# New order tables for a 32-batch graph-network kernel, and the timing rules of the recorder that carries them

## The chip, the cores and the metric

The kernel runs on one core of a Trainium2 chip. The metric is device time in microseconds (us) of one execution. A core has five engines that run side by side, each through its own instructions strictly in the order in which the program lists them: TensorE (PE in the profile; its weight loads are listed apart as PEld), VectorE (DVE), ScalarE (ACT), GpSimd (POOL) and SyncE (SP, here only a queue of transfers). An instruction waits until the data and the buffers it needs are ready; everything behind it on its engine waits too. So the order of the instructions on each engine decides how well the engines overlap.

## The reference

Four graph layers run one after the other on 32 independent graphs ("batches") of 512 nodes with 128 features. Each layer takes a layer norm and a ReLU of x, computes its update and adds it to x:

```python
h = jnp.maximum(_layernorm(x), 0.0)
# layer 0: for each node the maximum over its neighbours (adj is 0 or 1, some 16 of 512)
p, q = h @ (W1 - W2), h @ W2
x = x + max over j of relu(p[i] + q[j] + b) * adj[i, j]
# layer 1: four sub-layers; each aggregates along rows and along columns of adj
src_agg = l2norm(adj, 2) @ (nodes @ ws + bs)
dst_agg = l2norm(adj, 1).T @ (nodes @ wd + bd)
f = tanh(concat(src_agg, nodes @ wn + bn, dst_agg) @ wu + bu)
# layer 2: one normalised aggregation, out = adj_n @ (h @ weight) + bias
# layer 3: four times a GRU cell over m = adj.T @ (h @ weight[l])
r, z = sigmoid(...), sigmoid(...); n = tanh(xn + r * hn); h = (1 - z) * n + z * h
x = x + h * mask
```

## The kernel before

Every batch is worked on whole: 512 nodes are four tiles of 128 rows. `batch` (L1847) calls `load`, `prepare`, `gathers`, `layer1` and `layer23`; three functions of `FastWeights` (`first`, `rest`, `last`, L1218 to L1368) prepare the weights. The steps of a batch, with the names that the profile uses:

- `load` and `prepare`: x and the adjacency matrix (`af`) arrive by transfers of the ACT queue. VectorE checks the matrix (`junk`), takes the norm's statistics (`st`, `mv`, `rstd`, `shift`), GpSimd raises rstd to the power -1/2, ScalarE writes `xn`. ScalarE casts the matrix to bfloat16 (`ab`); TensorE transposes it in 16 bfloat16 matmuls (`pat`, 128 columns each), multiplies the features (`pq`) and makes running counts of the neighbours (`pc`), which ScalarE casts (`cc`) and four SP transfers for each tile rearrange (`ccd`). 16 more bfloat16 matmuls of 128 columns (`pkey`) make keys from which VectorE finds the first neighbours (`top`, `at8`), and from those the list `idx`.
- `gathers`: GpSimd issues 28 indirect transfers (`G`, and `gm` for the first of each tile) that fetch neighbours' rows; VectorE keeps the maximum (`gm`). For neighbours beyond the first seven VectorE makes one-hot rows (`oh`; in the first three batches ScalarE makes some, through `far`), TensorE multiplies (`pa`, 32 float32r matmuls of 512 columns) and VectorE keeps the maximum (`acc`). `px` transposes it back; GpSimd adds it to x (`x1`) and issues four loads of the matrix as float32r (`an`).
- `layer1` and `layer23`: the aggregations `pg` (104 float32r matmuls of 512 columns in a batch: each value is split into a high and a low part, `hi` and `lo`), the dense products in float32 (`pu`, `pk`, `phn`, `pxn`: 45 of 512 columns), float32 transposes (`pt`, `pf`, `px`, `ph`), and between them the chain of activations on ScalarE and elementwise work on VectorE and GpSimd (`zc`, `lo`, `shift`). The result `xo` is stored by the ACT queue.

The arithmetic is the same in every batch; only a few groups of operations are split in halves in the first and the last batch.

The order is not written out by hand. All those calls go through `Flow` (L826), which records an operation (`Op`) instead of issuing it, with a cost, an engine and what it depends on. `run` (L1090) gives each recorded operation a due time from a table, `queue_up` (L957) sorts the operations of each engine by due time, and `step` (L1012) then issues the heads of the five queues, one at a time, always the one that can start first by the recorder's own clock. Within an engine the order is therefore that of the due times alone. The recorder's costs decide only three other things: how the engines' instructions are interleaved while the program is built, which of the eight PSUM banks a tile gets (`Share`, L748), and where `clock` (L1062) puts filler: a bfloat16 matmul named `spin`, written where the recorder expects TensorE to idle for more than a microsecond[...].

The tables are text, two characters of difference of three-glyph numbers in hundredths of a microsecond. `FRONT` holds one row for each of the three weight functions and for batches 0 to 7; `MIDDLE` is one row, used for batches 8 to 21, each shifted by `PERIOD`; `BACK` holds batches 22 to 31. A row is a starting time and one number for every operation of that batch.

What the recorder assumes before the change: 0.06 us from one engine to another (`LAT`), 0.25 us more in front of a matmul (`LOAD`), 0.13 us for each semaphore beyond the first that a VectorE, ScalarE or GpSimd instruction has to wait for (`EVENT`), and a port that VectorE and GpSimd hold by turns for some operations (`port`). A matmul costs the same whatever stood before it.

Of the kernel before, what the change touches and what calls it, by code (L numbers as in the profile page):

```python
# [13 lines left out]
F32 = mybir.dt.float32  # L14
F32R = mybir.dt.float32r
# [10 lines left out]
P = 128  # L26
# [11 lines left out]
PERIOD = 81.7354  # L38
# [3 lines left out]
    450.09,  # L42
    (
        "!!!!WQ!+m!0U!/Z!<.!8c!47!2a!=<!@j!A#!Gg!^L!|h!z_!}5!|?#3@#6##DX#FW#JH#e)#xU#xa#y,#z(#vC#"
        "xl#y7#y=$$P#sM#yB#}O$#E$,y#z/#|%#|r$#K$-p#}2#~&$)Y$)v$/&$+K$,1$-b$4_$,]$-,$/0$0Z$2u$4:$5"
        "#$7>$@#$/<$/m$24$39$1+$2e$1=$1k$3j$=8$8Z$>n$1l$67$=i$>=$Qn$7Q$2&$:@$Db$<d$g-$;M$0=$4u$;M"
        "$?r$DQ$Dg%XB#])$2U$9T$9[$9b$:!$<h$6e$6l$6s$7t$85$8~$9;$9M$9i$:*$:~$?1$A9$C|$E>$FF$Hw$K&$"
        "LN$T|$MK$Sj$T/%>2$QU$W7$Md$S&$Tw$^2$V)$bH$XE$cW$Yf$dh$^b$hT$bx$kY$d7$lr$eR$nd$hw$q|$k}$w"
        "$$o6$yB$pD$|?$v,$~S$wG%#t$yf%&+$|b%,<$~v%+p%$:%.[%&M%0#%,_%5u%-z%6k%/?%9R%2V%=#%6<%>h$;_"
        "$>g$B/$@($C+$=R$Ce$H:$Et$Kn$>P$JB$Mp$LZ$O2$Ac$Lr$R@$Oy$S^$G#$P4$VR$SR$Wp$NP$Tp$X[$V$$YU$"  # L50
        "Pq$X2$ZN$Zk$[G$T?$]w$`|$^I$ah$^S$`J$bj$`b$cy$_]$e?$jr$i9$m|$`>$oW$p)$q+$r4$nx$w-$xb$wa${"
        "_$ps$x7$}5$|x$~h$|S$}y%$,%#*%%I$}r%%|%&M%(2%(_%!U%(N%)X%(l%*{%8`%8k%93%9>%?q%A3%Eb%EC%Hq"
        "%E#%-H%ID%9R%:O%#5${$%eH%dg%Oo%LD%L&%KH%Ko%N_%LX%Kh%Nf%Nx%O2%Q(%QS%TJ%Ts%U@%Uj%VC%Z-%iE%"
        "ct%ec%f)%gz%h?%eK%fJ%fy%gc%h@%ho%iA%iW%jl%en%f3%fb%g4%gK%hW%i*%o`%qn%k:%lK%t(%t~%v3%w>%w"
        "I%wT%w`%x7%xz%yI%{3%|!%|Q%}!%}:%}Q%}i&!%%zU%zs%{J%|:%~/%~F&!0&!G&#X&!_&!v&#q&%%&&K&(Z&(|"
        "&)V&)a&*%&,&&+7&-2&-x&.J&/3&/y&16&1e&3@&+M&-I&-a&.3&.b&1M&1|&31&4(&+e&+|&0;&27&3H&4X&5Y&"
        "6k&7t&89&8C&<]&=1&=s&>{&A,&Ab&Ay&BJ&C#&Cj&Ee&Mo&B4&Bb&C;&D,&DC&DZ&Dr&EB&H$&O$&O<&P6&QS&R"
        "f&Sw&Tr&V(&YZ&^W&_i&aH&bX&bo&c5&cc&h<&gq&h)&dO&iS&i1&iL&g(&jf&j{&l;&lP&mD&oG&lw&mm&o}&qL"
        "&p#&w8&wO&wg&w~&xU&xm&y(&}M($f(%d(%z(&4(&T(,O(+|(($((?(-J(-s(,q();(.2(.9(.+(+S(.R(.i(.K("
        "0!(28(3k(48(0;(4o(5W(5D(5O(5Z(5l(69(7>(89(93(9J(9b(9y(:4(:K(:c(:z(;K(<i(>%(=z(?7(@:(;W(>"  # L60
        "}(>n(@6(A2(A$(B%(Bn(Cx(D&(DI(Dl(E1(F%(Dw(Eq(G&(G>(GU(Gm(H((H?(HV(Hn(I?(KL(Lu(L^(N*(P`(IV"
        "(JQ(M|(OK(Pw(QQ(R?(S^(Un(Uy(V((W-(WN(X`(V3(WO(Y](Z.(ZE(Z](Zt([/([F([^(]/(_<(^B(`M(a-(c<("
        "`M(b/(a_(cR(dA(d5(e7(f!(gM(gX(gd(go(h4(i[(gz(i0(k$(k<(kS(kk(l=(lT(ll(m&(mT(nm(oh(o~(px(q"
        "q(ml(pb(pm(qs(ro(ra(sc(tO(uW(uc(un(uy(wn(wS(v>(w9(xE"
# [6 lines left out]
            "!!!!(?!(S!(+!(h!)7!!S!)X"  # L71
# [3 lines left out]
        2.69,  # L75
        (
            "!!Z!.r!1P!/F!2$!-m!2U!3*!3Z!4/!0|!4`!/w!54!5e!69!6j!0K!.A!:y!;>!=U!!B!<0!=O!<:!@:!B2!B^!"
            "<D!@D!!!!%Z!;(!;I!<(!<p!+N!<>!<`!==!>*!*m!=S!=u!>S!@N!>i!>j!?#!@<!?O!?O!?q!&m!;I!@D!@f!A"
            "P!B<!<`!Ag!BM!C+!CW!=u!CH!Cj!DH!Du!D^!D_!E%!FW!Fp!FB!G?!?O!@f!Fl!Fw!Go!IV!HW!JE!Bs!I5!I@"
            "!J*!K=!Lg!My!Cj!L!!Ki!LO!M8!M{!NJ!MN!MN!Me!N5!P%!Ny!Y=!FU!Gh!Q!!Q3!QO!Qz!S(!SR!Rn!T+!Im!"  # L80
            "SG!T#!T/!Un!Vb!Vx!W1!W^!LO!WR!WG!Wu!X:!Y.!Z*!Yp!ZV!YC!YD!YZ!Zh!Z*!ZF!Zs"
# [3 lines left out]
        4.33,  # L85
        (
            "!$G!(H!Y_!az!aX!b4!ao!bT!!!!ad!bT!b>!c*!*5!b)!bI!cf!d+!d{!fq!bv!il!ia!i#!jo!d+!jn!jy!k(!"
            "kI!l=!pC!j1!pE!p;!pP!pr!kI!r3!r>!r(!r`!t[!uW!pr!v|!w+!w6!xb!r`!y|!z+!z6!zW!{X#83!&m!|=!}"
            "q"
# [5 lines left out]
            "!!!!!M!#(!)z!*X!*2!+*!+!!*x!*Q!+I!+c!+y!+[!-3!.N!-K!.%!.x!.$!0p!1w!3:!4A!/E!/[!/r!0,!2e!"  # L95
            "27!32!4^!5p!65!2C!3=!6*!65!7,!2N!3H!5{!6A!8/!2Y!4j!6L!6W!:p!4u!8Y!9k!=Y!6c!7^!:0!:R!Ah!C"
            ".!Fb!Gi!:a!9T!<3!>2!@^!<u!?G!9l!=b!CM!GW!FR!JP!:&!Cd!H,!G&!MF!DH!=:!G1!Lk!_X!S3!I>!;w!<0"
            "!>&!>=!>S!>i!LS!5?!=Q!>O!>V!>^!>{!?g!?f!?m!?s!?z!@R!Ei!BU!B]!Bd!EH!He!K5!F{!G%!GC!GJ!L&!"
            "NG!Q8!T*!QM!GQ!R>!R_!Qf!Wp!TE!S7!US!`/!Vb!bu!X~!d~!Z0!eu!`_!i&!cI!k|!eQ!mv!fm!oK!iJ!qo!l"
            "C!tl!n=!vb!oo!x`!r~!{o!u2!}V!w(#!L!y%#$J!|6#(Z!}z#*H#!o#,7#$m#.5#(}#1~#+O#3t#,}#5I#.X#6}"  # L100
            "!J$!L-!Lr!Lq!MY!Le!N?!PB!P;!QW!J5!MF!PR!RC!Pj!S<!Nr!Pn!RV!Ux!Up!Vr!T2!V@!Wk!Vi!Xd!U;!W#!"
            "Y^!Ye!ZV!TK!VX!Z*![_!]G!_N!X?!Zg!]_!`P!]u!aI!^E!_v!c:!`1!d4!b7!c@!f:!cW!g3!^(!_x!co!h-!g"
            "f!i;!aG!c+!g}!k2!h8!lr!j)!kY!n.!kq!o`!l5!m>!pp!o&!r&!hF!ku!ps!s)!q-!s~!od!rG!tP!u8!th!vv"
            "!x/!x:!xE!yQ#7@#8r#;&#;e#:d#;E!$Z#<>!^Z!])![>!]p!_(!X<!Y+#?Y#?2#>+#?F#?y#?n#>J#@##@7#@L#"
            "@>#Ac#B,#Bc#C0#CX#D3#Dy!u1#C0#CY#DA#E*#EV#Eo#Fw#G(#G@#Gr#H/#H;#HT#K[#F+#G4#GL#GY#Gf#G~#H"
            "G#J!#M!#Ha#Hm#Hy#IA#IM#IY#If#Is#LO#J?#JK#JX#Je#Jq#LS#La#Lm#O@#M1#Nf#Mj#Nr#N:#P.#Pp#PY#Q)"
            "#Qk#Qp#Q{#R^#Ri#R@#T:#S.#SZ#S6#U(#U@#UY#Uf#Ur#V!#V;#Vm#SZ#U4#UM#V/#VG#VT#Va#Vm#Wo#Vy#W*#"
            "W6#WB#WO#W[#X!#X/#XR#X<#XH#XT#Xa#Xn#Xz#Y*#Y6#YY#YC#[1#YO#[=#Y{#Zb#[G#]E#]|#^b#]:#]q#_U#_"
            "a#_,#br#`$#b<#`%#c`#d)#dA#dM#dg#e!#e0#eR#`N#cl#cx#d5#ds#e<#eH#eU#e{#c3#dZ#eb#en#ez#f+#f7"
            "#fC#f~#c@#fO#f]#fi#fu#g$#g2#g>#h=#gJ#je#gW#jq#h&#k@#hR#kl#i)#l;#iT#j2#kV#lg#mD#n*#m~#n-#"  # L110
            "nz#o(#pG#q0#oI#pH#q1#qz#rM#rY#rg#rs#s/#sT#{k#qT#rA#s!#s<#sH#sb#sn#sz#ui#t*#t7#tC#tO#t[#t"
            "i#tu#v<#}4#u$#u1#vj#vv#w>#wJ#wV#wc#|o#z/$#c#|V$$j#}Y$%V#~)$&=#~T$(#$!$$(g$!P$)6$#7$*%$#o"
            "$$>$,A$*R$*~$-4$-5$-?$.($.2$2&$4s$4`$4K$3*$7Y$7K$7R$3I$9:$9g$9B$=>$=V$>v$>M$>#$@!$E?$Ah$"
            "A($GB$GY$Gq$H,$HC$HY$Hq$Ku$My$N3$N`$Nv$Sc$S}$OZ$RD$Uj$VC$T;$Rj$Vq$Vc$Vj$S-$W&$W=$Ww$XS$Y"
            "F$Zy$Xy$[F$[|$_)$]E$]W$]j$]u$^;$_F$`W$aR$aj$b$$b;$bR$bj$c$$c<$cj$e,$f%$f<$g7$h4$cv$gV$g4"
            "$hh$id$ld$kv$nm$ou$p#$q7$qB$qd$rs$p<$r_$sY$t-$tD$t[$ts$u.$uD$u[$v-$x?$yh$yO$zy$|!$v.$w9$"
            "zL${p$|`$}2$~^%!{%$C%$N%%T%%`%&#%(5%$Y%&$%)2%)a%)x%*2%*I%*a%*x%+3%+a%-q%,`%/%%-q%1i%.l%0"
            "A%0(%2)%2t%2z%3v%4b%5l%6q%6|%7+%7L%8?%5w%7e%9Y%9q%:,%:C%:r%;-%;D%;[%<?%=K%>E%>[%?V%@N%<."
            "%?@%?K%@Q%AM%A?%BA%C6%D?%DO%DZ%Df%H$%Gf%G1%GK%HM"
# [5 lines left out]
            "!*T!0>!0v!1.!1B!1w!1i!1p!1b!2:!2L!2c!2S!3y!5E!6f!4y!4B!=f!A#!C,!D+!FB!GZ!L#!L5!L@!]U!L/!"  # L125
            "LP!LV!L[!d{!LJ!Lb!Lg!Mm!f/!Ms!Mx!M~!NJ!h&!N4!ND!NO!Na!hz!dS!b.!rw!vL!e!!eN!kM!s<!tq!uJ!w"
            "5!xk!uH!lD!lr!pG!mV!n+!px!lk!nc!r5!tC!so!uy!mV!qz!zC!vM!tt!rf!o~!w|!zt!{y!{H!y:!jW!l-!o<"
            "!oQ!oh!qM!qc!G@!t4!t;!tB!tI!{_!~c!v5!v<!vB!vI!yK!z`!vP!vW!v_!vf!|y#!n!vm!y5!y<!yC##`#$]#"
            "*7#2|#*L!{<#$r#3[#9*#>4#:8#=%#-D#B7#/9#G-#0k#Ci#2B#F9#Bh#K0#G^#P<#Hy#QW#J+#S4#KR#Uh#P_#Y"
            "=#Qz#[8#SV#]]#V/#_S#Y`#c(#[[#e##^##g,#_v#ht#cK#kw#eF#mk#gN#os#i:#qu#l=#t|#n1#vU#p:#x_!}Y"  # L130
            "#!]#$@#$P#&K#%G#&P#(D#&h#)I!|b!~>#(!#*V#(G#-6#!]#%&#*E#/+#+E#0]#+7#0(#3&#1Y#3p#,@#1~#4i#"
            "2R#5b#*<#.,#3.#6[#4l#7T#/K#2B#5e#9P#6_#<M#;D#>o#?W#?V#@P#=.#@?#AI#AH#DB#3|#9J#D)#HD#G<#I"
            "0#:i#A8#HR#L%#LS#M$#E0#M)#O[#NB#PP#KD#OG#R1#Rg#U+#BV#NI#UI#U}#XK#YQ#Oh#Q&#Yk#ZJ#Z2#[M#]c"
            "#]n#]y#^(#x~#ym#{}#|@#{^#{?!!!#}2#,H#D{#+^#*s$*5$)S#xd$!Z#~z$!2$!F$#r$#d$#k$#]$$/$$D$$($"
            "%Z$%t$&g$(Y$)%$)]$*F$.1$)_$)j$)u$*#$*E$*`$,>$-V$.@$.o$/@$/o$0*$1]$,U$-($-?$-n$.)$/*$/W$3"
            "x$6p$0A$2%$2}$7x$:B$;K$;V$;y$<U$<w$=b$=v$?($?V$@)$@@$@V$@n$A@$An$>1$??$?n$A)$AW$Ao$B*$D,"
            "$Ew$DB$DY$El$G!$I.$J6$JA$JL$JW$Jy$LU$Kw$N%$N=$O&$P>$PU$Qo$R*$R~$L2$Mk$NT$Nl$OU$RA$SS$Te$"
            "UA$LI$La$Pt$RX$Sj$U5$VJ$WZ$Xd$Z@$ZK$^j$_>$`&$a|$co$d1$dH$d_$eO$e~$gi$qs$b>$dv$eg$f9$fP$f"
            "h$g!$h#$k-$lL$ld$uy$vt$x)$y#$zM${H$~{%%I%&Z%*q%*|%++%+6%+w%-e%0I%1>%,p%0B%1g%1n%.n%2u%34"
# [2193 lines left out]
```

## Time and profile before

| | us |
|---|---|
| median of 3 runs (2860.01 to 2862.24) | 2861.26 |
| the profiled execution | 2865.97 |
| its span, from the first to the last instruction | 2864.3 |
| PE, PEld busy | 2784.9, 1727.7 |
| DVE busy | 2491.5 |
| POOL, ACT busy | 1738.8, 1272.7 |

The numbers that follow come from the profiled execution, which took 4.7 us more than the median. "Busy" is the time in which at least one instruction of an engine was under way. Matmuls overlap in their pipeline, so the distance from one matmul's start to the next tells more of TensorE than the duration that a row gives. Nearly all operations are issued by one line, L1048 in `step`, so groups are told apart by the tiles that they write and read, not by line.

The batches leave the core at an even pace for most of the run: the stores of `xo` are issued at 284.5 us for batch 0 and at 2400.1 us for batch 25, which is 84.6 us for a batch, and at 2853.8 us for batch 31.

### The profile page before, as it was taken

The numbers are of one execution on the slowest core, as the hardware profiler recorded it, in microseconds if no ns is written. First come the engines' busy times: TensorE is split into PE (matmuls) and PEld (weight loads), VectorE is DVE, ScalarE is ACT, GpSimd is POOL, SyncE is SP. The second block draws the span as 40 slices with busy tenths as digits, with TensorE's granted clock in tenths as the row PEclk, the third lists the DMA queues.
The fourth block names the chain that finished last, engine by engine and source line by source line (L and its number), as shares of the span: only waits on it lengthen the run. The fifth ranks groups of instructions, "written<-read, shape, count | busy, mean of one in ns | idle before, by whom it ended". The sixth has DMA issues, their size and how long they took to land.

```text
span 2864.3 us, 37049 instructions
## 1 busy us (share of the span) xinstructions
PE 2784.9 (97%) x11230; PEld 1727.7 (60%) x11230; DVE 2491.5 (87%) x5757; ACT 1272.7 (44%) x2622; POOL 1738.8 (61%) x1892
## 2 busy tenths in 40 slices
PE   7899999999999999999999999999999999999997
PEld 4565656665666666566666666666655555656665
DVE  5889999999999999999999999999998998888633
ACT  5744444444444444444444444444444444444333
POOL 3676666666666676666666666666665666655311
PEclk8999999999999999999999999999999999999999
DMA  6654443434344343334343334434333434333100
GB/s 160 121 78 77 73 86 71 84 71 81 73 89 86 65 88 72 77 80 87 72 82 74 79 74 88 87 64 92 72 78 78 88 78 88 57 62 59 35 5 9
DMA packets 188178, 217.60 MB, mean 76 GB/s; under 512 B 28826, under 2 KB 136516, under 8 KB 187972
## 3 DMA queue, kind: packets, MB, share of 16 engines
q0 software_dynamic: 47104, 92.34, 24.4%
q1 hardware_dynamic: 73540, 64.62, 7.6%
q10 hardware_dynamic: 67328, 58.20, 6.6%
q8 instruction: 92, 1.51, 0.2%
q14 instruction: 114, 0.93, 0.1%
HBM read 164.32 MB, written 17.17 MB: 63 GB/s over the span
## 4 chain that ended last, share of the span: by engine, by line
PE 58%; DVE 19%; issue 9%; ACT 5%; POOL 4%; DMA 2%; SPq 1%; DVEq 0%; ACTq 0%; POOLq 0%
PE pg L1048 19%; PE pk L1048 11%; PE pu L1048 9%; DVE acc L1048 6%; PE pa L1048 5%; PE phn L1048 3%; DVE oh L1048 3%; PE pxn L1048 3%; DVE nn L1048 2%; POOL rstd L1048 2%; POOL G L1048 2%; DVE lo L1048 2%; PE ph L1048 1%; PE pf L1048 1%; ACT xn L1048 1%
## 5 line engine op out<-in xcount | busy, mean ns | idle before, releaser
L1048 POOL DMA_INDIRECT G<-qtab,idx x768 | 829.7, 1080 | 522.0 <-DVE gm L1048 259.3
L1048 DVE TENSOR_TENSOR acc<-acc,pa 128x512 f32<-128x512 f32 x992 | 672.9, 678 | 66.6 <-PE pa L1048 44.2
L1048 PE MATMUL pa<-oh,qhl 128*128 128x512 f32 x1024 | 535.3, 548 | 6.1 <-DVE acc L1048 2.1
L1048 PE MATMUL pu<-ag,w 128*128 128x512 f32 (+1 forms) x952 | 452.9, 572 | 0.0
L1048 PE MATMUL pg<-an,hi 128*128 128x512 f32 (+1 forms) x1072 | 446.5, 418 | 0.4 <-DVE lo L1048 0.4
L1048 PE MATMUL pg<-an,lo 128*128 128x512 f32 (+1 forms) x1072 | 428.0, 405 | 0.3
L1048 DVE TENSOR_SCALAR oh<-ccd 128x1024 fp32r<-128x1024 bf16 x492 | 374.5, 771 | 2.8 <-PE pa L1048 1.5
L1048 ACT ACTIVATE xn<-x,shift,rstd 128x128 f32<-128x128 f32 x512 | 223.5, 485 | 221.3 <-POOL shift L1048 211.0
L1048 PE MATMUL pg<-at,hi 128*128 128x512 f32 (+1 forms) x672 | 291.5, 441 | 2.3 <-ACT oh L1048 1.4
L1048 PEld LDWEIGHTS pa<-oh,qhl 128*128 128x128 f32 x1024 | 193.6, 191 | 144.1 <-issue 68.2
L1048 PE MATMUL pg<-at,lo 128*128 128x512 f32 (+1 forms) x672 | 278.9, 418 | 1.0 <-POOL lo L1048 0.8
L1048 POOL TENSOR_TENSOR rstd<-rstd,mhalf 128x4 f32<-128x4 f32 x128 | 190.4, 1488 | 109.5 <-DVE rstd L1048 92.1
L1048 ACT ACTIVATE gate<-pk,bsum 128x512 f32<-128x512 f32 (+1 forms) x264 | 174.6, 674 | 180.1 <-PE pk L1048 178.6
L1048 PE MATMUL pk<-h,g_hh 128*128 128x512 f32 (+1 forms) x528 | 253.3, 585 | 0.7 <-ACT h L1048 0.7
L1048 PE MATMUL pk<-mT,g_ih 128*128 128x512 f32 (+1 forms) x528 | 252.8, 583 | 0.4 <-ACT mT L1048 0.3
L1048 DVE TENSOR_TENSOR gm<-gm,G 128x128 f32<-128x128 f32 x768 | 244.0, 319 | 7.4 <-DMA G<-qtab,idx 6.3
L1048 PEld LDWEIGHTS pu<-ag,w 128*128 128x128 f32 x952 | 171.5, 190 | 123.1 <-issue 96.0
L1048 PEld LDWEIGHTS pg<-an,lo 128*128 128x128 f32 x1072 | 202.8, 189 | 65.2 <-issue 28.2
L1048 PEld LDWEIGHTS pg<-an,hi 128*128 128x128 f32 x1072 | 202.9, 189 | 64.8 <-issue 24.9
L1048 ACT COPY mT<-pg 128x512 f32<-128x512 f32 (+1 forms) x164 | 94.4, 576 | 319.3 <-PE pg L1048 311.4
L1048 POOL DMA_INDIRECT gm<-qtab,idx x128 | 133.3, 1041 | 99.7 <-issue 86.2
L1048 DVE TENSOR_TENSOR ag<-pg,rbc 128x512 f32<-128x512 f32 (+1 forms) x272 | 174.9, 646 | 21.2 <-PE pg L1048 17.8
(177 smaller groups left out, 5241.8 us busy)
## 6 DMA issues: line engine op xcount, KB each, us to landing
ccd<-cc SPq DMA_DIRECT2D x512, 64.0 KB
an<-in_adj_dram POOLq DMA_DIRECT2D x128, 256.0 KB
af<-in_adj_dram ACTq DMA_DIRECT2D x31, 1024.0 KB
x<-in_x_dram ACTq DMA_DIRECT2D x64, 256.0 KB
rbc<-scal SPq DMA_DIRECT2D x32, 512.0 KB
G<-qtab,idx POOLq DMA_INDIRECT x768
qtab<-qn SPq DMA_DIRECT2D x32, 256.0 KB
out_dram<-xo ACTq DMA_DIRECT2D x32, 256.0 KB
```

What stands on the lines that cost most here:

```text
L1048: op.fn(*(real(v) for v in op.args), **{k: real(v) for k, v in op.kw.items()})
```

## The change

The arithmetic and the recorded operations stay as they are. All due-time tables are replaced, and the recorder's assumptions are:

```diff
-PERIOD = 81.7354
+PERIOD = 81.7343
...
-    LAT = 0.06
-    LOAD = 0.25
+    LAT = {"pe": 0.035, "vec": 0.035, "act": 0.035, "pool": 0.09, "sync": 0.035}
+    LOAD = (0.08, 0.09, 0.14, 0.2)
+    SWITCH = {(1, 2): 0.066, (0, 2): 0.006, (3, 2): 0.006}
...
-    EVENT = 0.13
+    YIELD = 0.12
...
+                wide = self.name == "pool" and op == "tensor_scalar" and outs[0].free_size() >= P
+                self.flow.part[-1].port = fast or wide or len(tensors) > 1
+            if self.name == "pool" and (op.startswith("tensor") or "indirect" in op):
+                self.flow.part[-1].kind = not self.flow.part[-1].port
...
         if "pool" in at and ops["pool"].port:
             at["pool"] = max(at["pool"], self.port["vec"])
+        elif "pool" in at and ops["pool"].kind:
+            at["pool"] = max(at["pool"], self.port["vec"] - self.YIELD)
...
-        cost = op.cost + (self.EVENT * max(0, len(need) - 1) if op.engine != "pe" else 0.0)
+        cost = op.cost
         if op.engine == "pe":
-            cost /= self.rate
+            cost = (cost + self.SWITCH.get((self.kind, op.kind), 0.0)) / self.rate
+            self.kind = op.kind
```

Every matmul now carries a kind (0 float32 transpose, 1 bfloat16, 2 float32r, 3 float32), and a float32r matmul behind a bfloat16 one is counted with 0.066 us more. A GpSimd instruction that takes no turn at the port is nevertheless held back until 0.12 us before VectorE gives the port up. Some costs change by a few hundredths (an SP transfer of bfloat16 0.6 instead of 0.48, an indirect transfer 1.0 instead of 1.05, operations on half the partitions 0.11 more, an accumulating ScalarE operation 0.1 less).

The tables have one row more in `FRONT` (batches 0 to 8), `MIDDLE` covers batches 9 to 21, `BACK` has the same ten batches. The order is different on every engine, in all batches. Counted in the order of the built programs:

| | before | after |
|---|---|---|
| matmuls without fillers | 9960 | 9960 |
| VectorE, GpSimd, SP instructions | 6765, 1930, 811 | 6765, 1930, 811 |
| `spin` fillers, all | 209 | 128 |
| `spin` fillers up to the output of batch 0 | 127 | 73 |
| bfloat16 matmul followed by a float32r one, all | 408 | 56 |
| the same in one inner batch | 14 | 1 |
| float32r matmul followed by a bfloat16 one, all | 379 | 136 |
| the same in one inner batch | 12 | 4 |

In an inner batch the 32 bfloat16 matmuls stood mostly one by one among float32r aggregations; in the new order they stand next to float32 products and float32 transposes. At the start, the preparation of layer 1's weights (`wt`, `pwt`, `pw`, and the SP loads that feed it) stood between the steps of batch 0, and now comes after more of them: the SP queue writes all 16 `ccd` pieces of batch 0 before it goes on with those weights, where weight loads stood between the pieces before, and on GpSimd the first `an` load comes after two gathers instead of after eight. ScalarE issues one instruction more in the whole program (3068 instead of 3067): one more load of an activation table, since `low` of the weights now comes behind batch 0's `xn` and `hT`.

## The prediction

> **What bounds the kernel now.** I read the page's busy shares first, then busy time by stretches, then TensorE's timeline from start to start, then the waits.
>
> ```profile
> span 2864.3 us, 37049 instructions
> ...
> PE 2784.9 (97%) x11230; PEld 1727.7 (60%) x11230; DVE 2491.5 (87%) x5757; ACT 1272.7 (44%) x2622; POOL 1738.8 (61%) x1892
> ```
>
> TensorE is busy 97% of the time, VectorE 87%, so TensorE is the bound. But a busy share of overlapping matmuls hides lost time, so I price TensorE's work by distances between starts. Stretches of one batch's length, two of them inner:
>
> ```profile
> core 0: us, PE busy (x) PEld busy (x) DVE busy (x) ACT busy (x) POOL busy (x), PEclk, DMA share, GB/s
> 0.00:84.10 84.10, 62.46 (x290) 38.51 (x290) 52.00 (x141) 52.08 (x120) 34.11 (x74) 0.86 0.61 154
> 84.10:168.20 84.10, 70.51 (x379) 47.86 (x378) 70.44 (x180) 51.41 (x95) 58.95 (x68) 0.94 0.68 110
> ...
> 925.10:1009.20 84.10, 83.80 (x333) 51.53 (x331) 77.98 (x179) 37.64 (x79) 55.00 (x59) 1.00 0.40 79
> 1513.80:1597.90 84.10, 83.80 (x333) 51.60 (x332) 78.10 (x179) 37.65 (x78) 55.05 (x59) 1.00 0.41 79
> ...
> 2775.30:2859.40 84.10, 69.49 (x332) 46.74 (x330) 33.43 (x94) 28.65 (x62) 10.64 (x17) 0.98 0.03 7
> ```
>
> The inner batches repeat to a tenth of a microsecond, and only the first two stretches and the last leave TensorE really idle. Now two places on TensorE's timeline, each with one short matmul among float32r ones:
>
> ```profile
> 1500.00 0.40 PE L1048 MATMUL pa<-oh,qhl 128*128 128x512 f32 x1
> 1500.24 0.23 PE L1048 MATMUL pkey<-ltk,at 128*128 128x128 bf16 x1
> 1500.28 0.48 PE L1048 MATMUL pg<-at,hi 128*128 128x512 f32 x1
> 1500.60 0.39 PE L1048 MATMUL pg<-at,lo 128*128 128x512 f32 x1
> ...
> 1533.80 0.27 PE L1048 MATMUL pt<-ident,xn 128*128 128x128 f32 x1
> 1533.83 0.48 PE L1048 MATMUL pa<-oh,qhl 128*128 128x512 f32 x1
> 1534.14 0.40 PE L1048 MATMUL pg<-at,hi 128*128 128x512 f32 x1
> ```
>
> Float32r matmuls follow each other every 0.23 us. A float32 transpose costs 0.109 (transposes in a row start 109 ns apart), and transpose plus float32r matmul take 1534.14 - 1533.80 = 0.34: nothing extra. A bfloat16 matmul costs 0.056, yet with the float32r one behind it takes 1500.60 - 1500.24 = 0.36, where 0.056 + 0.232 = 0.288 was due.
>
> By such distances an inner batch is: 144 float32r of 512 columns at 0.232 us, 33.4; 45 float32 of 512 at 0.858 (two records of 0.429 each), 38.6; 49 transposes at 0.109, 5.3; 32 bfloat16 at 0.056, 1.8; four `pq` at 0.432 and four `po` at 0.222, 2.6. Sum 81.7. Between the stores of batch 0 and batch 25 a batch takes (2400.1 - 284.5)/25 = 84.6, so 2.9 are lost in each.
>
> With the same prices TensorE's order holds 181 us of work up to batch 0's output, which is stored at 284.5: 103 lost in filling. After batch 25's store come 453.7 us with 411 of work: 43 lost. Losses: 103 + 73 + 43 = 219.
>
> **What the Trainium skill says.** "Perfetto Trace Analysis", Identifying the Most-Contended Engine, says that matmul busy share is a bad measure because pipelined matmuls distort it; the trace agrees, 83.80 of 84.10 us busy beside 81.7 of work. "TensorE: Matmul & The Clock Gate", Back-to-back issue gap, gives an isolated gap of N/2.4 + 2.5 ns: 56 ns for 128 columns, as bfloat16 shows here; for 512 columns 216 ns, while float32r shows 232. I found no section on the cost of changing the type between matmuls, so that price is the trace's alone. "SBUF — State Buffer", Who interferes with whom, says that VectorE and GpSimd share a port pair as an exclusive lock, which an operation of VectorE with two SBUF inputs takes against a GpSimd operation that reads SBUF. The trace fits:
>
> ```profile
> POOL G L1048 <- DVE gm L1048: 259.3, 244, 4.5
> ```
>
> GpSimd's gathers are held 244 times behind `gm`, a maximum of two SBUF tiles; part of that may be plain buffer waits.
>
> **The change part by part.**
>
> The type switch. Over the 207 places in which bfloat16, float32r, float32r follow each other, the median from the first start to the third is 0.352, so a switch costs 0.352 - 0.288 = 0.064. The way back, float32r to bfloat16 to float32, takes 0.306 where 0.288 was due: 0.018. In all, 408 - 56 = 352 switches go (22.5 us) and 379 - 136 = 243 ways back (4.4): 26.9 us. For an inner batch this is 13 x 0.064 + 8 x 0.018 = 0.98, so 24 us over the 25 batches between the two stores, 2.5 in the end stage. It is paid on the bound engine and no other work hides it. What the bfloat16 matmuls stand beside now, float32 and transposes, costs nothing extra: bfloat16 then float32 is 0.541 to the second half, 0.056 + 0.429 + 0.056 at most.
>
> TensorE's other waits in the inner batches. Of the 2.9, the old switches take 14 x 0.064 + 12 x 0.018 = 1.1; 1.8 remain, small waits that recur at the same places (`pf` for `f`, `pt` for `xn`, `pa` for `oh`; in most batches 1.3) and about 1 us more every few batches. A new order built on nearer durations can move consumers behind their operands. The old allowances differ from the trace: VectorE behind TensorE starts 39 ns after the recorded end, ScalarE behind VectorE 34, GpSimd behind ScalarE 90, where 60 was assumed. The new ones are 35 and 90. Bounds: all 1.8 gone (-45 us) or none (0), or worse than now, which the rivals take. I take 0.96 gone for each batch, 24 us: the old order had planned none of these waits, so some misfit will remain.
>
> Filling. Weights' preparation is moved behind the first steps of batch 0. That takes `pw` and its waits out of the early path:
>
> ```profile
> PE pw L1048 <- ACT wt L1048: 4.6, 8, 1.2
> ```
>
> TensorE's work ahead of batch 0's `px` falls from 32.3 to 20.5 us. But VectorE's ahead of that maximum grows from 68.5 to 79.3 us, as batch 1 is begun earlier, and it was reached at 109.7, so VectorE was idle 41 us there; GpSimd's work ahead of `x1` grows from 65.6 to 67.7. The gathers (28 at some 1.04 us), not the weights, still pace batch 0. Between the first `pg` and the last transpose of layer 1 in batch 0, TensorE gets 40.3 us of work instead of 45.8. Moves on SP count too: 16 `ccd` transfers pass the weight loads, which then land later, before they are used in layer 1. The added table load costs 1.28 us by its row and stands ahead of `ab`. 54 fewer fillers free nothing, since they stood in idle time. Sum: -5.5 for layer 1, about -4 for the early path, +1.3: 8 saved. Bounds: 25 saved (a quarter of the 103) and 12 lost.
>
> The end. The last batch's serial chain is ordered alike. I take the switches' 2.5 and 3 for waits, 5.5 (0 to 12).
>
> The recorder's constants issue nothing. Their only effects outside the order are banks and fillers, priced above. GpSimd's holding-back is the recorder's bookkeeping, not an instruction; VectorE waited for gathers only 7.4 us in the whole run, so better knowledge of that port is worth little in itself.
>
> Sum: 24 + 24 + 8 + 5.5 = 62. The profiled execution, 2865.97, becomes 2804; the median lies 4.7 lower: 2799. Own range: from all inner waits gone and a good filling (2861 - 24 - 45 - 20 = 2772) to a third of that gain (2822).
>
> **The rivals.**
>
> *Switches only.* Waits and filling stay. For it: the counts are certain, everything else is estimated. Against it: the same waits recur at the same places, so they can be ordered away. 2861 - 27 = 2834.
>
> *VectorE takes over.* It is busy 78.0 of 84.1 us in an inner batch and waits 6.1 (`nn` for `gate` 1.2, `acc` for `pa` 1.1, `lo` for `hi` 1.1, the rest in short gaps). If these waits stay, a batch still takes 84.1, and only 0.5 x 25, 8 and 5.5 are won: 2861 - 26 = 2835; with a few new ones, 2848. Against it: they are waits for TensorE and ScalarE, which would be earlier.
>
> *Slower: too tight.* The allowance between an operand and its matmul falls from 0.31 to 0.115 to 0.235 us, and 0.13 for further semaphores is dropped. About 45 groups of matmuls in a batch begin on a fresh operand of another engine. If half come 0.1 us late, that is 2.2 for each batch, against the switches' 0.98, with the old 1.8 still there: 25 x 1.2 = 30, less 8: 2883. It decides from 1.3 us of new waits in a batch on. Against it: the measured handoffs above match the new allowances.
>
> That the order doesn't change is excluded by the counts.
>
> **How the numbers follow.** Forecast 0.64, switches only 0.15, VectorE 0.12, too tight 0.07, no change 0.02. Differences of 0.2% (6 us) can't be told from none. Range 2770 to 2845: it holds nearly all of the forecast, switches only, and half of VectorE's case. Faster 0.89, same 0.03, slower 0.08.
>
> **What would show it.** Float32r behind bfloat16 should be rare and the rest of the pairs unchanged in distance. The pace between the stores of batch 0 and 25 should be 84.6 - 1.94 = 82.7 us; 83.6 means switches only; above 84.6 the tight order. Batch 0's store should come near 276, batch 25's near 2343, and 448 us should follow it to the last. VectorE's waits in an inner batch should fall to about 4. I am wrong if the gain lies mainly in the filling, or if VectorE's idle time is as large as before and TensorE waits for `nn` and `lo`.

## The result: no gain, and the profile after

| | before | after |
|---|---|---|
| median, 13 runs of each (us) | 2860.01 | 2865.99 |
| ratio, 95% interval | | 1.0022 (1.0013 to 1.0030) |
| span of the profiled execution | 2864.3 | 2866.4 |
| store of batch 0 | 284.5 | 280.6 |
| from there to batch 3 | 254.9 | 260.8 |
| batch 3 to 8 | 420.5 | 420.9 |
| batch 8 to 21 | 1096.9 | 1095.4 |
| batch 21 to 25 | 343.2 | 348.6 |
| batch 25 to 31 | 453.7 | 449.8 |
| median distance of two stores, batches 9 to 20 | 84.16 | 84.20 |

The new order is 0.2% slower where 2.2% faster was forecast. The rows of the profiles add up to 2.4 us, less than the 6.0 between the medians: the profiled execution of before took 6.0 us more than its median, that of after 2.1. The start gives 4 us and the end 4 us; two stretches, from the store of batch 0 to that of batch 3 and from batch 21 to batch 25, take 11; and an inner batch takes what it took. The page of after, and its busy time by stretches (columns as in the prediction):

```profile
span 2866.4 us, 36823 instructions
...
PE 2760.5 (96%) x11149; PEld 1748.4 (61%) x11149; DVE 2468.7 (86%) x5757; ACT 1269.0 (44%) x2623; POOL 1711.1 (60%) x1892
```

```profile
core 0: us, PE busy (x) PEld busy (x) DVE busy (x) ACT busy (x) POOL busy (x), PEclk, DMA share, GB/s
0.00:84.10 84.10, 60.18 (x264) 34.83 (x264) 65.23 (x175) 58.27 (x127) 43.83 (x87) 0.84 0.76 173
84.10:168.20 84.10, 75.08 (x408) 57.90 (x409) 63.75 (x160) 48.81 (x97) 54.77 (x59) 0.96 0.61 112
...
1513.80:1597.90 84.10, 83.19 (x333) 52.40 (x332) 76.93 (x179) 37.50 (x79) 54.04 (x59) 1.00 0.39 79
...
2775.30:2859.40 84.10, 70.89 (x333) 50.64 (x331) 36.23 (x100) 29.16 (x63) 10.69 (x17) 0.96 0.02 7
```

In the inner batch TensorE has become idle by 0.6 us more (83.80 to 83.19 busy) and VectorE by 1.2 more (78.10 to 76.93): both wait for something else. The switches are gone as planned: at the 159 places of after where a bfloat16 matmul and two float32 halves follow each other, the third start comes 0.541 us after the first (median), as the prediction had it. By the prediction's own prices an inner batch of after is 81.77 us of work (its sum of 81.7, less rounded) and 0.14 of switches, which leaves 2.3 of the median distance for waits; before it was 81.77, 1.11 and 1.3. What the switches gave, new waits took. They stand at few places: `pt` for `xn` 0.47 us, `pf` for `f` 0.47, `pa` for `sct` 0.35, `ph` for `h` 0.32. The experiments below trace all four to one engine, GpSimd. The chain of waits of after, followed back from a later batch (start, duration, piece):

```profile
1563.34 0.69 DVE lo L1081
...
1566.53 2.94 POOL G L1081
1569.48 1.20 POOL an L1081 x2
...
1570.97 1.05 POOL G L1081
1572.02 1.08 POOL rstd L1081
...
1573.76 1.65 ACT xn L1081 x4
...
1575.44 0.52 ACT hi L1081
...
1575.97 0.69 ACT f L1081
...
1576.70 0.55 PE pf L1081 x3
```

One gather takes 2.94 us; its neighbours take 0.95 to 1.05. GpSimd is late from there on, `shift` with it, ScalarE waits with `xn`, `f` stands behind `xn` on ScalarE's queue, and TensorE waits for `f`. The gather and the one ahead of it in GpSimd's timeline, then what VectorE did meanwhile:

```profile
1565.28 0.95 POOL L1081 DMA_INDIRECT G<-qtab,idx  x1 [3.38 <-DVE gm L1081]
1566.53 2.94 POOL L1081 DMA_INDIRECT G<-qtab,idx  x1 [0.30 <-DVE st L1081]
```

```profile
1566.18 0.29 DVE L1081 BATCH_NORM_STATS2 st<-x 128x6 f32<-128x128 f32 x1
1566.38 2.28 DVE L1081 SCALAR_TENSOR_TENSOR junk<-af 128x2048 bf16<-128x2048 f32 x1
```

`junk` is the check that the adjacency matrix holds only 0 and 1. It reads two operands from SBUF (both are the matrix), takes 2.28 us, started 0.15 us before the gather, and the gather ended 0.8 us after it. The same was to be seen in the trace of before, at the same place of the batch, with another victim. GpSimd's timeline of before, and VectorE's:

```profile
1565.78 1.04 POOL L1048 DMA_INDIRECT G<-qtab,idx  x1 [0.17 <-issue]
1567.21 3.01 POOL L1048 TENSOR_TENSOR rstd<-rstd,mhalf 128x4 f32<-128x4 f32 x1 [0.39 <-issue]
1570.31 0.20 POOL L1048 TENSOR_TENSOR shift<-shift,rstd 128x4 f32<-128x4 f32 x1
```

```profile
1566.96 0.16 DVE L1048 TENSOR_SCALAR rstd<-mv 128x4 f32<-128x4 f32 x1
1567.04 2.28 DVE L1048 SCALAR_TENSOR_TENSOR junk<-af 128x2048 bf16<-128x2048 f32 x1
```

`rstd` needs 1.05 us elsewhere. Such a hold doesn't appear among the waits: it lies inside the duration of the instruction that is held. It is no accident of one batch: of the 15 checks between 630 and 1830 us, 14 in before have an `rstd` of 3.0 us starting 0.18 us behind them, and 14 in after a gather of 2.9 starting 0.15 to 0.17 us behind. Both orders lose about 1.9 us of GpSimd once in a batch to it.

### The profile page after: what moved, and what is told of

Its sections match the earlier page's. It is cut to its first block, busy times and chain, and to the rows that moved or that the text cites. A ratio compares the mean times of both kernels' runs of the same rounds, so it can differ in the third digit from the quotient of the medians.

```text
span 2866.4 us, 36823 instructions
## 1 busy us (share of the span) xinstructions
PE 2760.5 (96%) x11149; PEld 1748.4 (61%) x11149; DVE 2468.7 (86%) x5757; ACT 1269.0 (44%) x2623; POOL 1711.1 (60%) x1892
## 4 chain that ended last, share of the span: by engine, by line
PE 51%; DVE 17%; POOL 14%; issue 8%; ACT 6%; DMA 3%; SPq 1%; ACTq 0%; DVEq 0%; POOLq 0%
PE pg L1081 17%; PE pk L1081 9%; PE pu L1081 9%; POOL G L1081 7%; PE pa L1081 5%; DVE nn L1081 4%; POOL gm L1081 3%; DVE acc L1081 3%; PE phn L1081 3%; ACT xn L1081 2%; PE pxn L1081 2%; DVE oh L1081 2%; PE ph L1081 2%; POOL rstd L1081 2%; PE pf L1081 1%
## 5 line engine op out<-in xcount | busy, mean ns | idle before, releaser
L1081 POOL DMA_INDIRECT G<-qtab,idx x768 | 859.6, 1119 | 622.4 <-DVE gm L1081 489.5
L1081 PE MATMUL pa<-oh,qhl 128*128 128x512 f32 x1024 | 477.2, 496 | 14.0 <-DVE acc L1081 7.3
L1081 PE MATMUL pu<-ag,w 128*128 128x512 f32 (+1 forms) x952 | 447.1, 574 | 4.4 <-DVE ag L1081 4.4
L1081 DVE TENSOR_SCALAR oh<-ccd 128x1024 fp32r<-128x1024 bf16 x492 | 351.9, 728 | 2.4 <-PE pa L1081 2.1
L1081 PE MATMUL pg<-at,hi 128*128 128x512 f32 (+1 forms) x672 | 276.0, 418 | 1.9 <-ACT hi L1081 1.9
L1081 PE MATMUL pg<-at,lo 128*128 128x512 f32 (+1 forms) x672 | 271.5, 406 | 0.6 <-POOL lo L1081 0.6
L1081 POOL TENSOR_TENSOR rstd<-rstd,mhalf 128x4 f32<-128x4 f32 x128 | 141.4, 1104 | 81.7 <-DVE rstd L1081 46.8
```

The costliest lines, as they stand in the source:

```text
L1081: op.fn(*(real(v) for v in op.args), **{k: real(v) for k, v in op.kw.items()})
```

## The experiments

The moves are made just before the queues are sorted: an operation's due time is set to that of another plus or minus 0.0001 us, so that it stands directly behind or ahead of it on its engine. Ratios are against the kernel before, run beside each; 1.0022 is the number to compare with for the new order.

**The matrix check without a second operand.** VectorE is busy for as long as before, but reads one operand, and writes 8 values of a row instead of 2048; the kernel leaves out the check:

```diff
-F.vec.scalar_tensor_tensor(junk, af2, 1.0, af2, ALU.is_equal, ALU.not_equal, accum_out=bad[:, b : b + 1])
+nc.vector.max(out=junk[:, 0:16].bitcast(F32), in_=af2)   # all of bad set to 0 at the start
```

> The order of after, with VectorE's matrix check junk (2.28 us, two SBUF operands) replaced in its place by a MAX8 over the same 2048 columns, one operand, about the same time on VectorE. The check of the matrix is left out. Port theory: while junk runs, GpSimd stands still (one gather takes 2.94 us instead of 0.95, once in a batch); its lateness reaches TensorE through shift, xn and f at pf and makes 1.1 of the 2.4 us that a batch loses. Then the long gather goes, the wait of pf falls from 0.47 to under 0.1 us, the pace from 84.15 to about 83.0 us and the time to about 2840 us (2830 to 2848). Rival, VectorE's sum of work or TensorE's waits in general set the pace: VectorE has as much to do as before, 2863 to 2868. Rival, something outside the order holds both kernels at 84.14 us a batch: unchanged.

> The same replacement in the order of before; the check of the matrix is left out. Port theory: rstd on GpSimd, 3.01 us behind junk, falls to 1.05, the wait of pf (0.35 us, and the drift ahead of it) goes, about 0.75 us a batch: some 2841 us (2834 to 2850), so that the two orders again differ little. If the new order is better wherever junk does not disturb it: after gains 1.0 us a batch more than before does. Rival, VectorE or an outside limit sets the pace: 2858 to 2862.

Measured: 2843.4 us after, ratio 0.9945 (0.9929 to 0.9962); 2838.5 before, 0.9923 (0.9906 to 0.9939). The replacement took 2.28 us on VectorE as the check did, and neither a gather nor an `rstd` took over 2.0 us in either kernel. The median distance of two stores fell from 84.20 to 83.10 and from 84.16 to 83.32. So the hold costs the old order 0.84 us a batch and the new one 1.10, VectorE's sum of work doesn't set the pace, and nothing outside of the two orders fixes 84.2: that both had the same pace is a coincidence of sums. Whether the second operand or the longer output makes the hold, this run doesn't tell. Without the hold the new order is better by 0.22 us in an inner batch, not by the 1.0 of its switches, and still 4.9 us slower over the run: batches 0 to 3 take 259.6 us beside 252.5, batches 21 to 25 take 348.1 beside 340.7.

**The same check in four pieces.**

```diff
-scalar_tensor_tensor(junk, af2, 1.0, af2, ..., accum_out=bad[:, b : b + 1])
+for k in range(4):
+    s = slice(512 * k, 512 * (k + 1))
+    scalar_tensor_tensor(junk[:, s], af2[:, s], 1.0, af2[:, s], ..., accum_out=(a column of its own))
```

> The order of after, with junk issued as four instructions of 512 columns each in its place: the same check, but VectorE gives its port up three times in between, at about 0.25 us more of VectorE's time. Port theory: the gather behind it is held 0.6 us at most instead of 1.9, about 0.9 us a batch are won and up to 0.25 given back: 2845 us (2838 to 2855). If GpSimd cannot take the port between VectorE's instructions in a row, the gather is held as long as now: 2864 to 2872. Rival, VectorE sets the pace: 2866 plus 0.25 x 26, 2872 us.

> The same four pieces in the order of before. Port theory: rstd is held 0.6 us at most instead of 1.9: 2848 us (2840 to 2857). If GpSimd cannot take the port in between: 2859 to 2866. Rival, VectorE sets the pace: 2866 us.

Measured: 2848.2 us after, 0.9958 (0.9944 to 0.9972); 2841.1 before, 0.9935 (0.9918 to 0.9951); distances 83.16 and 83.35. GpSimd's timeline of the old order with the check in pieces, then VectorE's:

```profile
1551.78 1.41 POOL L1048 TENSOR_TENSOR rstd<-rstd,mhalf 128x4 f32<-128x4 f32 x1 [0.41 <-DVE rstd L1048]
1553.27 0.30 POOL L1048 TENSOR_TENSOR shift<-shift,rstd 128x4 f32<-128x4 f32 x1
```

```profile
1551.60 0.69 DVE L1104 SCALAR_TENSOR_TENSOR junk<-af 128x512 bf16<-128x512 f32 x1
...
1552.21 0.69 DVE L1104 SCALAR_TENSOR_TENSOR junk<-af 128x512 bf16<-128x512 f32 x1
...
1552.82 0.69 DVE L1104 SCALAR_TENSOR_TENSOR junk<-af 128x512 bf16<-128x512 f32 x1
```

`rstd` now begins under the first piece and ends under the third, 1.0 us after the second began: GpSimd gets in where one of VectorE's instructions ends. 3.01 us became 1.41. The pieces start 0.61 us apart, so the check takes 2.44 us of VectorE from its start to that of the next instruction, instead of 2.21, and that cost nothing that shows.

**The check three instructions later.**

```diff
+for b in range(10, 25):
+    named("vec", f"junk_{b}").due = named("vec", f"mv_{b - 4}_3").due + 0.0001
```

> The order of after with the matrix check junk some 0.9 us later on VectorE in batches 10 to 24 (behind the last mv of layer 3's norm), in one piece; nothing else moves. If GpSimd's gather loses the port by a narrow margin (it starts 0.15 us after junk), it is now first: it takes about 1 us instead of 2.94, and what is held behind junk is the next gather, by 0.6 us or so. Then pf's wait shrinks and the pace falls from 84.15 to 83.2 to 83.6: 2853 to 2859 us. If only the length of the hold counts, wherever it stands, 2864 to 2868.

Measured: 2853.4 us, 0.9969 (0.9958 to 0.9980), distance 83.17. The edit put `junk` behind the second of the four `mv`, not behind the last: one `gm` and two `mv` went ahead of it, some 0.35 us, less than the expectation said. It was enough. GpSimd's timeline, then VectorE's:

```profile
1554.46 0.95 POOL L1081 DMA_INDIRECT G<-qtab,idx  x1 [0.30 <-DVE st L1081]
1555.41 1.20 POOL L1081 DMA_DIRECT2D an<-in_adj_dram  x2
1556.91 1.05 POOL L1081 DMA_INDIRECT G<-qtab,idx  x1 [0.30 <-DVE junk L1081]
1558.08 1.04 POOL L1081 TENSOR_TENSOR rstd<-rstd,mhalf 128x4 f32<-128x4 f32 x1
```

```profile
1554.65 2.26 DVE L1081 SCALAR_TENSOR_TENSOR junk<-af 128x2048 bf16<-128x2048 f32 x1
```

Now the gather is first by 0.19 us and takes 0.95; the two loads `an` fill the time of the check, and the next gather follows it. Three short instructions put ahead of a long one, in 15 of 32 batches, are worth 0.5% of the run.

**The switches, put back and taken out.** On TensorE alone, each bfloat16 matmul goes to the nearest place within a limit that lies between two float32r ones (new order), or that has no float32r one behind it (old order):

```diff
+rest = q[:i] + q[i + 1 :]
+op.due = rest[j].due - 0.0001     # new order: rest[j - 1] and rest[j] float32r, within 1.2 us
+                                  # old order: rest[j] not float32r, earlier, within 4 us
```

> The order of after with bfloat16 matmuls of the inner batches put back between two float32r ones, at most 1.2 us from their places, on TensorE alone: 199 changes from bfloat16 to float32r instead of 56, 247 ways back instead of 136. By the prices of the prediction 143 x 0.064 + 111 x 0.018 = 11.2 us more work on TensorE. If a switch costs what it was priced at and TensorE's work is what counts: 2877 us. If TensorE's waits for GpSimd's late chain take it up: 2866 to 2870. If the price of the switch was wrong, distances between bfloat16 and the second float32r start stay below 0.30.

> The order of before with the bfloat16 matmuls between some 700 and 2000 us taken out from between float32r ones, at most 4 us earlier, on TensorE alone: 221 changes to float32r instead of 408, 256 ways back instead of 379. By the prices of the prediction 187 x 0.064 + 123 x 0.018 = 14.2 us less. If the prediction's switches-only term holds in full: 2846 us. If the wait for GpSimd (rstd behind the matrix check) takes it back: 2853 to 2860, with longer waits of pf for f. Slower than 2861 would mean that an earlier bfloat16 matmul waits for its operand or its bank.

Measured: 2875.9 us after, 1.0041 (1.0028 to 1.0053); 2854.0 before, 0.9968 (0.9957 to 0.9979). Put back, the distance of two stores rose from 84.20 to 84.80, 0.60 for nine switches and seven ways back more in an inner batch, priced at 0.70. Taken out, it fell from 84.16 to 83.43, 0.73 for twelve and eight, priced at 0.91. So 80 to 86% of the price shows in the inner batches, and TensorE's waits don't take it up, in either order: time on TensorE and time lost to GpSimd lie one behind the other. Over the whole run the gain was 9 of 14.2 us, the loss some 5 of 11.2 (1.0041 beside 1.0022), less than the prices; the distances of the inner batches are the cleaner measure.

**What else GpSimd's lateness costs the new order.** The check in four pieces, and `shift` of layer 1 two gathers earlier:

```diff
+for b in range(8, 22):
+    named("pool", f"shift_{b}_1").due = named("pool", f"G_{b + 1}_3_1").due - 0.0001
```

> The order of after with the matrix check in four pieces (2848 us when run alone), and on GpSimd shift of layer 1 issued two gathers earlier in batches 8 to 21. If the wait of pa for sct (0.39 us in each batch) is GpSimd's lateness, handed on by xn on ScalarE, it goes: 0.35 x 14 = 5 us, 2843 us, the pace near 82.75. If VectorE or the rest of the order takes its place: 2846 to 2850.

Measured: 2840.8 us, 0.9919 (0.9902 to 0.9935), distance 82.63 instead of 83.16: the wait of `pa` for `sct` was GpSimd's lateness too.

The last of the four waits, `ph` for `h`, begins where GpSimd holds VectorE. VectorE's timeline of after, then GpSimd's:

```profile
1543.03 1.29 DVE L1081 TENSOR_TENSOR gm<-gm,G 128x128 f32<-128x128 f32 x1
1544.24 0.68 DVE L1081 TENSOR_SCALAR oh<-ccd 128x1024 fp32r<-128x1024 bf16 x1
```

```profile
1542.91 1.26 POOL L1081 TENSOR_TENSOR x<-x,b 128x512 f32<-128x512 f32 x1 [0.21 <-ACT xn L1081]
```

GpSimd's addition is 0.12 us ahead and `gm` ends just behind it, 1.0 us late. First that addition (of layer 2's bias to `x2`) is made in four pieces, on top of the run above; then, in place of the pieces, the kernel leaves it out in all batches:

> As the run with the earlier shift, and in all batches GpSimd's addition to x2 (128x512, 1.26 us) in four pieces of 128 columns. If this addition holds VectorE's gm for 1.0 us and so makes the wait of ph for h (0.34 us a batch), gm falls from 1.29 to about 0.6 us and the wait goes: 0.3 x 26 = 8 us less than the run with the earlier shift. If the four pieces cost GpSimd more than they free, or VectorE cannot get in between: no change or up to 5 us slower.

> As the run with the check in four pieces and the earlier shift (2841 us, pace 82.6), with GpSimd's addition of the bias to x2 left out in all batches (its four-piece form did not help). If this addition, which takes the port 0.12 us ahead of VectorE's gm, makes gm 1.29 us long and ph wait 0.35 us for h, both go: pace 82.25, about 9 us less over the run, 2832 us. If the wait of ph has another cause: 2839 to 2842.

In pieces: 2844.5 us, 0.9934 (0.9918 to 0.9951), no gain; the four took 1.75 us, and VectorE's `gm` and the `oh` behind it were still held for 1.1 together. Left out: 2831.1 us, 0.9884 (0.9867 to 0.9900), distance 82.35; the longest `gm<-gm,G` of an inner batch was 0.51 us. The wait of `ph` is gone. Of these 10 us a part may be GpSimd's saved work; the 0.28 of each inner batch fits the wait of 0.32.

**One instruction in the start.** Near 185 us GpSimd's `lo` of batch 0 held VectorE's `gm` for 1.90 us, and TensorE waited 3.2:

```diff
+named("pool", "lo_0_2").due = named("pool", "rstd_5_0").due + 0.0001
```

> The order of after with a single GpSimd instruction moved: lo of batch 0's layer 2 behind the rstd that follows it (near 185.6 us). There GpSimd's addition to x2 (2.44 us, itself held by the matrix check) and this lo hold VectorE's gm for 1.38 and 1.90 us, ag comes late, TensorE waits 3.2 us and then works at half pace for some 5 us. If this chain makes the loss of the batches 0 to 3 (260.8 us between their stores, 254.9 before), the second gm falls to about 0.3 us, TensorE waits 1.5 us less, its granted clock between 170 and 200 us rises from 0.83 to above 0.90, and the three batches take 256 to 258 us: 2861 to 2864 us. If the next wait takes its place: 260 us and 2866.

Measured: 2863.8 us, 1.0006 (0.9998 to 1.0015). The granted clock is the last figure but two, in the stretches of after and of this run:

```profile
170.00:200.00 30.00, 24.62 (x89) 14.86 (x88) 23.61 (x60) 15.51 (x34) 20.63 (x23) 0.83 0.29 67
```

```profile
170.00:200.00 30.00, 26.18 (x102) 15.70 (x103) 25.59 (x66) 16.19 (x35) 24.16 (x27) 0.94 0.32 67
```

The chain was right: `gm` fell to 0.25 us, TensorE's wait to 1.6, and the clock stayed up. The place was not: batch 0 was stored at 277.0 instead of 280.6, while from there to batch 3 it took 260.8 as in the new order without this edit. What these lose is something else.

**Both gains in the old order.** The check in four pieces and the switches taken out:

> The order of before with both edits that gained alone: the matrix check in four pieces (ratio 0.9935) and the bfloat16 matmuls between 700 and 2000 us taken out from between float32r ones (0.9968). If the two act on different losses, they multiply: 0.9903, 2833 us beside 2861. If TensorE's switches and GpSimd's hold lie on parallel chains, less: 2838 to 2841.

Measured: 2832.2 us, 0.9891 (0.9875 to 0.9908), distance 82.62: 1.54 less than before, where 0.81 and 0.73 alone make 1.54. The two losses are separate, and their gains add up. This version, with the whole computation, is 1.1% faster than the kernel before and 1.3% faster than the new order.

## Why the prediction was wrong

- **Switches, 24 us in the inner batches: right, and given back.** The count fell, and the price held to 80% (taken out) and 86% (put back), which makes some 20 of the 24 us, an estimate from these two runs.
- **TensorE's other waits in the inner batches, 24 us gone: this step failed.** The prediction took 0.96 of 1.8 us a batch as gone because the new durations are nearer to the trace. In an inner batch the waits rose instead, from 1.3 to 2.3 us. (The 1.8 is a mean over 25 batches and holds the edges too: before took 343.2 us from batch 21 to 25, where four inner distances make 336.6.) Three causes on GpSimd make most of the waits: taken away one after the other, they brought 84.20 down to 83.16, 82.63 and 82.35, 1.85 in all.
- **"Better knowledge of that port is worth little in itself": the root of it.** The prediction priced the port by VectorE's waits for gathers, 7.4 us in the run, and read GpSimd's 244 waits behind `gm` as a sign of it. Waits of either kind end with a semaphore and don't show a hold. The cost lay inside durations, of `rstd` in before (3.01 us beside 1.05, in 14 of 15 inner batches, worth 0.84 us of pace), of a gather and of `gm` in after. The trace of before had it, with `junk` 0.17 us ahead in the next row of another engine. The Trainium skill, "SBUF — State Buffer", Who interferes with whom, which the prediction cites for `gm`, says that the loser of the port blocks for the whole instruction of the other; read against the longest VectorE instruction with two inputs it points to `junk`.
- **The removed constants "issue nothing": true of the instructions; what they did for the tables stays open.** A gather counts 1.0 us in the new recorder, and a further semaphore that it waits for nothing. In the trace two gathers in a row start 1.25 us apart (1565.28 and 1566.53 above). Less than 0.2 us decides who holds whom for 1 or 2 us. That the new order's margins were too small is read from the starts (0.15 and 0.12 us in after), and shown for the check by moving it; that the constants made them so was not tested.
- **Filling, 8 us: 4**, and another 3.7 lay in one `lo`. **The end, 5.5: 3.9.** One bound of the range is also a sum that doesn't come out: a third of the gain from 2861 to 2772 leads to 2831 us, not to 2822.
- **Rivals.** "Too tight" had the right sign and nearly its threshold (1.3 us of new waits a batch; 1.0 came), but another mechanism: not half of 45 matmul groups late by 0.1 us each, but four places late by 0.3 to 0.5. Its mark, more than 84.6 us between the stores of batch 0 and 25, was met too, with 85.0, but by the two long stretches and not by the inner batches. "VectorE takes over" falls: its idle time grew, and a check 0.23 us longer on VectorE made the kernel faster.
- **Two stretches, 11 us, were in no case.** TensorE's wait for `h` of layer 3's cell is the largest there. All of it in the waits of before, then of after (us in total, times, longest):

```profile
PE ph L1048 <- DVE h L1048: 8.9, 12, 1.3
```

```profile
PE ph L1081 <- DVE h L1081: 26.5, 39, 2.2
```

Between the stores of batches 0 and 3 it rose from nearly nothing to 4.7 us, between those of 21 and 25 from 0.6 to 6.0. Some of it looks like the same hold: at 447.81 us VectorE's `nn` ahead of such an `h` takes 1.76 us, where the others take 0.68, and GpSimd's `lo` started 0.07 us before it. Most of these waits show no such instruction. Why `h` is late there stays open: the one experiment aimed at the first stretch hit another loss.

## What to carry to other kernels

Before an order is tuned by hundredths, list for each kind of instruction the longest duration beside the median: here an instruction three times as long as its like was held, and what held it ran on the other engine at that moment. Where an order is packed so tightly that a small error of a price decides which of two engines comes first, give long instructions that hold the other engine a margin, or cut them into pieces, before squeezing the bound engine. And price a gain on the bound engine together with the waits behind it: here the two gains of 0.81 and 0.73 us a batch added up to 1.54.

## What the runs showed of the hardware

- A gather that had started 0.19 us before `junk` ran in 0.95 us, and `junk` took 2.26: neither held the other. One that started 0.15 us after it took 2.94. The Trainium skill, "SBUF — State Buffer", Who interferes with whom, has whoever is first keep the port for the whole instruction while the other blocks; here the two overlapped for 0.76 us and neither took longer than alone, and the measurement decides.
- Loads issued by GpSimd (`an`, two in 1.20 us) were not held while `junk` ran.
- GpSimd gets in between VectorE's instructions in a row (`rstd` 1.41 us across three pieces), while VectorE was still held for 1.1 us by four GpSimd additions in a row (1.75 us).
- A VectorE instruction of the same length with one operand and a short output did not hold GpSimd: with MAX8 (2.28 us) no gather exceeded 2.0 us, where the check made one of 2.94 in most batches of after.
